# Gated delta rule in a two-layer decoder: beta and g computed inside the feed-forward, closing norms inside the schedule, a longer lookahead, and 32-wide TensorE tiles

## The chip, the cores and the metric

The kernel runs on one core of a Trainium2 chip. The engines of that core that matter here are TensorE (PE in the profile, and PEld for its weight loads), VectorE (DVE), ScalarE (ACT), GpSimd (POOL) and SyncE (SP). SP issues nearly all DMA transfers, and its queue is issued in order. The metric is the device time of one execution in microseconds, lower is better. An engine executes its own instructions in the order in which the program lists them, so a waiting instruction holds up what stands behind it on the same engine.

## The reference

Two decoder layers on `x` of shape (32, 64, 256), 2048 tokens of 256 numbers, all in float32. Each of six blocks adds its result to `x` and normalises the sum:

```python
x = _layernorm(x + _L0_attn_ref(x, ...))    # lightning attention
x = _layernorm(x + _L0_xattn_ref(x, ctx, ...))  # banded attention
x = _layernorm(x + _L0_ffn_ref(x, ...))     # feed-forward of 1024, its own layernorm inside
x = _layernorm(x + _L1_attn_ref(x, ...))    # gated delta rule
x = _layernorm(x + _L1_xattn_ref(x, ctx, ctx, ...))
x = _layernorm(x + _L1_ffn_ref(x, ...))     # 64 experts, 8 for each token
```

The change lies in the third and the fourth block. The feed-forward computes `relu(x @ up) ** 2 @ down`, adds `x @ expert` scaled by the sum of the two largest of eight logits, and normalises. The delta rule has 16 key heads and 32 value heads of 128 columns, and runs on chunks of 64 tokens; a sequence of the reshaped input is 64 tokens long too, so every chunk is a sequence and starts from a zero state:

```python
beta = sigmoid(x @ w_b)                       # 32 numbers for each token
g = -exp(a_log) * softplus(x @ w_a + dt_bias)  # 32 numbers for each token
q, k, v = split(silu(causal_conv4(x @ w_qkv)))
z = x @ w_z
# for each sequence of 64 tokens and each value head
g = cumsum(g)
decay = exp(g[i] - g[j]) for i >= j, else 0
A = -(beta * l2norm(k)) @ l2norm(k).T * decay   (strictly lower)
T = inverse(I - A)                              (64 x 64, unit lower triangular)
out = (l2norm(q) / sqrt(128) @ l2norm(k).T * decay) @ T @ (v * beta)
out = out * rsqrt(mean(out ** 2)) * norm_w * silu(z)
x_new = concat(out over heads) @ w_out
```

## The kernel before

`x` stays on the chip through the whole kernel as 16 tiles of 128 tokens; four of these tiles make a chunk `c` (512 tokens, eight sequences), of which there are four. The stages run one after the other; in the profiled execution the first attention takes 0 to 375 us, the banded attention 375 to 737, the feed-forward 737 to about 891, the delta rule with its prologue 885 to 2594, the second cross attention with the routing 2596 to 3160, and the experts the rest.

**Feed-forward (L664 to L708).** For each chunk, `make_xT` transposes `x` on TensorE (eight transposes, two ScalarE copies) into `xT[c]`; eight pairs of matmuls make `ph`, ScalarE takes its relu, GpSimd squares it into `hT` (L683). Then, for each of the four tiles, `pe` (L689) and `py` follow on TensorE, and VectorE and ScalarE combine them. Two layernorms (`x<-x,mv,rstd` is L176) close the chunk. VectorE, ScalarE and GpSimd need some microseconds for that after the last matmul; the next chunk's `make_xT` and `ph` need only their own tiles of `x`.

**Prologue of the delta rule (L711 to L808).** Constants are loaded, the two DRAM scratch buffers `tudram` are filled with zeros by SP, `make_xT` is done for all four chunks, and then beta and g are computed for all 16 tiles at once: `pba` (L770, 32 matmuls), ScalarE and VectorE element by element on 128x512, `pc` (L791, the cumulative sum), `pgT` (the same transposed), and SP stores the latter into the DRAM scratch `gdram`, from which the loop reads it back as rows to broadcast.

**Loop (L810 to L1197).** There are 64 steps, 16 key heads by four chunks. A step `s` consists of generators, each yielding before each piece of work the engine and the microseconds that the piece is expected to take:

- `conv` (L832 to L865): four of them for each step. `pp` (L850, two matmuls of 128x512), ScalarE's `acc` (L854), three VectorE additions (L859), ScalarE's silu. A first conv of a step needs step `s-5` or `s-6` done. At the first chunk of a key head SP loads its weights `wqkv`, `wz`, `wo` (two buffers).
- `decay` (for two steps at once): SP broadcasts g from `gdram`, GpSimd and ScalarE make the decay matrix.
- `matrices`: GpSimd squares (`sq`, L903), `pn` (L910, sums of squares as 32-wide matmuls of one column), VectorE's `ssum` (L916), `pk` (k with k and q), VectorE makes `am` (A transposed) and `at`; SP stores `am` to `adram`, and for each pair of steps loads the 16x16 diagonal blocks back as `w`.
- `value`: `pv` (transposes), scaled by ScalarE.
- `invert` (for two steps at once): VectorE inverts the 16x16 blocks; SP stores them into the diagonal of `tudram` (two scratch buffers), whose remaining entries are the zero fill, and then loads them back as whole 64x64 matrices `tu`, which hold T and its transpose U (four loads a step, four buffers).
- `gate`: `pz` (L1047) and ScalarE's silu.
- `delta` (L1055 to L1105): doubles the inverse twice, 16 to 32 and 32 to 64. `per_sequence` (L1067) issues one 64x64 matmul for each of 8 units and 2 sequences; the tile of a sequence lies on 64 rows and 64 columns of the array. Level one: `px` = A T, VectorE copies its lower block into `xi` (L1085, an identity otherwise), `ptu` = U xi, ScalarE copies it into T (L1090). Level two: `px` and `pm`, the product of T with `at`, VectorE copies `xi` (L1097), ScalarE `mt` (L1100), then `pm2` from `xi` and `mt`, and ScalarE's copy (L1105).
- `output` (L1108 to L1146): `po` (L1118, weights of 64 rows and 128 columns), ScalarE's square, VectorE's product with the gate, `pso`, and a power on GpSimd (L1144).
- `project` (L1148 to L1171): `py` (L1158) with the output weights, added to `x` (L1165, L1167, L1169). It sets the step done.

**What sets the order.** `scheduled` (L41 to L110) runs all of these as streams when the program is built. Each stream has so many items open at once; an item waits for its named events ("need") that others set. Of the items it can start, the function takes the engine whose next start is earliest by the costs that the generators give, and within 0.3 us prefers the stream listed first. The order that comes out is the order of each engine's instructions. Two rings stand for the PSUM banks: two for the convs, six for the rest; every "+" takes one, every "-" gives one back. `LEVELS` is (16, 32).

**After the loop (L1198 to L1205)** four layernorms, one for each chunk, and four SP stores to `xq`, from which the next stage loads its queries.

`pss` (L344) is a matmul of the first attention.

Of the kernel before, what the change touches and what calls it, by code (L numbers as in the profile page):

```python
# [23 lines left out]
LEVELS = (16, 32)  # L24
# [96 lines left out]
def decoder_kernel(ctx: ExitStack, tc: tile.TileContext, d, out):  # L121
# [539 lines left out]

    with tc.tile_pool(name="f0", bufs=1) as wp, tc.tile_pool(name="f0w", bufs=2) as sb, tc.tile_pool(
# [9 lines left out]
        for c in range(NCH):  # L672
            make_xT(c, ps)
            hT = sb.tile([P, 8, 512], FP, name="hT", tag="hT")
            for f in range(8):
# [7 lines left out]
                nc.gpsimd.tensor_tensor(hT[:, f, :], hr, hr, ALU.mult)  # L683
            ys = []
# [26 lines left out]
    with tc.tile_pool(name="g1", bufs=1) as wp, tc.tile_pool(  # L711
# [6 lines left out]
        id64 = load(wp, d["c_id64"], [P, S], "id64")  # L718
        low = load(wp, d["c_low"], [P, S], "low")
        lvl = wp.tile([P, 2, S], U8, name="lvl")  # L720
# [4 lines left out]
        adram = [dp.tile([2, 2, 8, PITCH], FP, name=f"adram{i}") for i in range(2)]  # L725
        tudram = [dp.tile([2, 2, 2, 8, PITCH], FP, name=f"tudram{i}") for i in range(2)]
        gdram = dp.tile([16, NCH, 2, 4, 2, S], FP, name="gdram")
        gall = wp.tile([P, NT, 32], FP, name="gall")

        wo16 = [wp.tile([P, 2, 16, 16], FP, name=f"wo16{i}") for i in range(2)]  # L730
        xis = [[wp.tile([P, 8, S], FP, name=f"xi{l}{i}") for i in range(2)] for l in range(2)]
        for i in range(2):
            nc.sync.dma_start(out=wo16[i].rearrange("p o j e -> p o (j e)"), in_=d["c_wid"].rearrange("p (o x) -> p o x", o=2))
        for xs_ in xis:
            for t in xs_:
                nc.gpsimd.tensor_copy(t, over(id64, 8))
# [5 lines left out]
        for c in range(NCH):  # L742
            make_xT(c, ps)


        beta = wp.tile([P, NT, 32], FP, name="beta")
        with tc.tile_pool(name="g1l", bufs=1) as tmp:
            lvlf = load(tmp, d["c_lvl"].rearrange("p (l i) -> p l i", l=2), [P, 2, S], "lvlf")
# [9 lines left out]
            tri = load(tmp, d["c_tri"], [P, P], "tri")  # L758
            wba = load(tmp, d["w_ba"].rearrange("(k p) e -> p k e", p=P), [P, 2, 64], "wba")
            dtb = load(tmp, d["dt_bias"].to_broadcast([P, 32]), [P, 32], "dtb")  # L760
            alog = load(tmp, d["a_log"].to_broadcast([P, 32]), [P, 32], "alog")
            g = tmp.tile([P, NT, 32], FP, name="g")
            aa = tmp.tile([P, NT, 32], FP, name="aa")
            ab = tmp.tile([P, NT, 32], FP, name="ab")
            for t8 in range(2):
                pba = ps.tile([P, 8, 64], FP, name="pba", tag="ps")
                for k8 in range(8):
                    t = 8 * t8 + k8
# [266 lines left out]
        def gate(s, h):  # L1035

            kh, c = steps[s]
            if h == 0:
                yield "need", ("done", s - 3)
                gates[s] = sb.tile([P, 2, 512], FP, name="z", tag="z", bufs=3)  # L1040
# [473 lines left out]
```

## Time and profile before

| quantity | value |
|---|---|
| median of 17 executions | 3691.15 us (3681.33 to 3710.32) |
| profiled execution, own time | 3693.18 us |
| profiled execution, span | 3691.5 us |
| mean granted TensorE clock over the span | 0.933 |
| PE busy | 3365.6 us (91%) |
| PE weight loads (beside PE) | 2154.2 us (58%) |
| VectorE busy | 2105.5 us (57%) |
| ScalarE busy | 1384.6 us (38%) |
| GpSimd busy | 1525.5 us (41%) |

The profile is of one execution; the medians are over executions without a profile. A line of it names the source line, the engine, the operation, output and inputs by the program's names, the size of the weights and of the stream for a matmul, the count, the busy time, the mean time of one, and the idle time of the engine just ahead of these instructions with what released them. A float32 matmul leaves two records, so counts of matmuls are twice those in the source. Ends of matmuls are modelled in the trace, so a sum over rows can exceed the time in which PE was busy. The granted clock is the share of full speed that the hardware gave TensorE. A view by windows gives the busy time of each engine for a stretch of the span.

### The profile page before, as it was taken

What the parts mean: (1) busy time and instruction counts of PE and PEld (TensorE: products, weight loads), DVE (VectorE), ACT (ScalarE), POOL (GpSimd) and SP (SyncE); (2) the same over time, 40 slices, a digit from 0 to 9 for tenths busy, and PEclk for the clock granted to TensorE, in tenths of its full rate; (3) what the DMA queues carried; (4) which work ended last, traced back from release to release, by engine and by line L of the source; (5) the groups of instructions that cost most, each with busy time, mean ns of one, the idle gap of its engine ahead of it and who ended that gap; (6) DMA issues with size and microseconds to landing.
All of it is one profiled execution on the core that took longest, in us unless ns stands there. A gap on an engine that the chain in (4) does not pass through costs nothing.

```text
span 3691.5 us, 91942 instructions
## 1 busy us (share of the span) xinstructions
PE 3365.6 (91%) x39042; PEld 2154.2 (58%) x39042; DVE 2105.5 (57%) x4316; ACT 1384.6 (38%) x2422; POOL 1525.5 (41%) x1779
## 2 busy tenths in 40 slices
PE   9999999897799999999999999999788888599990
PEld 4667566565376666766666666767444444355550
DVE  4333555544667677676677777675655555233337
ACT  1110333321545455554555555454222222133330
POOL 3322344443434344443444434443333333466663
PEclk9999899997899999998999999999878788799995
DMA  9910111001323233332332333322111111466655
GB/s 316 383 24 16 40 33 33 20 29 37 82 51 69 47 66 66 59 67 53 65 59 58 68 59 60 64 56 50 46 38 44 47 33 38 132 211 216 214 180 213
DMA packets 538700, 317.80 MB, mean 86 GB/s; under 512 B 420145, under 2 KB 498737, under 8 KB 531889
## 3 DMA queue, kind: packets, MB, share of 16 engines
q1 hardware_dynamic: 517680, 259.32, 27.3%
q0 software_dynamic: 18432, 50.49, 3.7%
q8 instruction: 308, 5.05, 0.6%
q10 hardware_dynamic: 2176, 2.10, 0.2%
q14 instruction: 104, 0.84, 0.1%
HBM read 166.42 MB, written 137.00 MB: 82 GB/s over the span
## 4 chain that ended last, share of the span: by engine, by line
PE 75%; DVE 9%; issue 5%; POOL 5%; ACT 3%; DMA 1%; another core or an unknown queue 1%; SPq 1%; POOLq 0%; DVEq 0%; ACTq 0%
PE pp L850 11%; PE py L1158 6%; PE po L531 6%; PE pz L1047 5%; PE pq L296 4%; PE sc L467 4%; PE pm L1067 3%; PE po L1118 3%; PE px L1067 3%; PE sc L499 3%; PE py L384 3%; PE py L1372 3%; PE pg L1362 2%; PE pu L1362 2%; PE ptu L1067 2%
## 5 line engine op out<-in xcount | busy, mean ns | idle before, releaser
L859 DVE SCALAR_TENSOR_TENSOR acc<-pp,cw,acc 128x504 f32<-128x504 f32 (+2 forms) x768 | 556.7, 731 | 189.4 <-ACT acc L854 159.8
L850 PE MATMUL pp<-xT,wqkv 128*128 128x512 f32 x1024 | 504.6, 618 | 22.9 <-DMA wqkv<-in_w_qkv_dram 11.7
L509 ACT ACTIVATE eT<-sc 128x768 f32<-128x768 f32 (+1 forms) x256 | 222.4, 915 | 348.0 <-PE sc L499 232.8
L477 DVE TENSOR_REDUCE mext<-sc 128x4 f32<-128x768 f32 (+1 forms) x256 | 267.6, 1087 | 101.3 <-PE sc L467 69.3
L204 POOL DMA_INDIRECT ybuf<-ye,xe x256 | 246.2, 962 | 175.7 <-DVE ye L1376 93.9
L903 POOL TENSOR_TENSOR sq<-kq 128x512 f32<-128x512 f32 x128 | 134.5, 1053 | 436.8 <-ACT kq L864 332.4
L850 PEld LDWEIGHTS pp<-xT,wqkv 128*128 128x128 f32 x1024 | 185.3, 194 | 185.6 <-issue 167.5
L1169 POOL TENSOR_TENSOR x<-x,y 128x256 f32<-128x256 f32 x256 | 184.6, 728 | 252.3 <-DVE x L1167 244.7
L467 PE MATMUL sc<-k,q 32*128 32x192 f32 (+1 forms) x2048 | 219.4, 428 | 60.4 <-issue 50.3
L1158 PE MATMUL py<-wo,og 128*128 128x256 f32 x1024 | 261.0, 393 | 2.2 <-DVE x L1167 2.2
L854 ACT ACTIVATE acc<-pp,cw 128x512 f32<-128x512 f32 x256 | 175.4, 687 | 233.5 <-PE pp L850 232.9
L1047 PE MATMUL pz<-xT,wz 128*128 128x512 f32 x512 | 246.1, 601 | 0.0
L1158 PEld LDWEIGHTS py<-wo,og 128*128 128x128 f32 x1024 | 186.9, 192 | 43.8 <-issue 16.7
L518 POOL TENSOR_SCALAR_AFFINE_SELECT eT<-eT 128x256 f32<-128x256 f32 (+1 forms) x256 | 127.6, 534 | 204.2 <-ACT eT L509 204.1
L467 PEld LDWEIGHTS sc<-k,q 32*128 32x128 f32 x2048 | 125.9, 206 | 119.5 <-issue 93.6
L531 PE MATMUL po<-eT,va 128*32 128x192 f32 (+1 forms) x2048 | 183.5, 404 | 6.5 <-issue 3.3
L499 PE MATMUL sc<-qb,k 32*128 32x192 f32 (+1 forms) x2048 | 165.3, 387 | 14.4 <-DVE mext L477 11.2
L1365 DVE TENSOR_TENSOR hT<-hT,pu 96x512 f32<-96x512 f32 x64 | 43.7, 683 | 235.5 <-PE pu L1362 224.1
L1167 DVE SCALAR_TENSOR_TENSOR x<-py,ro,x 128x256 f32<-128x256 f32 x256 | 122.5, 480 | 96.1 <-ACT y L1165 94.4
L531 PE MATMUL po<-eT,one 128*32 128x192 f32 (+1 forms) x2048 | 175.6, 389 | 0.9 <-issue 0.7
L1144 POOL TENSOR_TENSOR ro<-gvar,mhalf 128x8 f32<-128x8 f32 x64 | 105.3, 1646 | 145.2 <-DVE gvar L1139 138.1
L1165 ACT ACTIVATE y<-py,ro 128x256 f32<-128x256 f32 x256 | 120.8, 474 | 113.9 <-PE py L1158 105.7
(226 smaller groups left out, 6514.4 us busy)
## 6 DMA issues: line engine op xcount, KB each, us to landing
xbuf<-zero SPq DMA_DIRECT2D x32, 1032.0 KB
xe<-xbuf SPq DMA_DIRECT2D x64, 516.0 KB
tu<-tudram SPq DMA_DIRECT2D x256, 128.0 KB
ybuf<-zero SPq DMA_DIRECT2D x16, 1024.0 KB
de<-gdram SPq DMA_DIRECT2D x64, 256.0 KB
adram<-am SPq DMA_DIRECT2D x128, 128.0 KB
yk<-ybuf SPq DMA_DIRECT2D x16, 1024.0 KB
kk<-kT SPq DMA_DIRECT2D x32, 256.0 KB
```

What stands on the lines that cost most here:

```text
L204: i = nc.gpsimd.indirect_dma_start(out=dst, out_offset=bass.IndirectOffsetOnAxis(ap=rows, axis=0), in_=src, in_offset=None).ins
L467: nc.tensor.matmul(sc[ng // 2][:, ng % 2, qt * W : (qt + 1) * W], q32[rows, r, qt * P : (qt + 1) * P], k32[rows, r, lo[qt] : lo[qt] + W], ...
L477: nc.vector.tensor_reduce(mv4[:, 2 * hf : 2 * hf + 2, :, 8], sc[hf][:, :, : 2 * W].rearrange("p j (q l) -> p j q l", l=W), AX.X, ALU.max, ...
L499: nc.tensor.matmul(sc[ng // 2][:, ng % 2, lt * W : (lt + 1) * W], k32[rows, r, lt * P : (lt + 1) * P], qb[rows, lo[lt] : lo[lt] + W], star ...
L509: nc.scalar.activation(eT[:, 2 * hf : 2 * hf + 2].rearrange("p j h q -> p j (h q)"), sc[hf][:, :, : 2 * W], AF.Exp, scale=float(1 / np.sqr ...
L531: nc.tensor.matmul(po[32 * ng : 32 * ng + 32, i, lo[lt] : lo[lt] + W], one8[:, r, :] if i else va[:, lt, ng, 32 * r : 32 * r + 32], eT[:, ...
L850: nc.tensor.matmul(pp, weights[kh][0][:, k, i, :], xT[c][:, k, :], start=k == 0, stop=k == 1)
L859: nc.vector.scalar_tensor_tensor(acc3[:, :, sh:], pp3[:, :, : S - sh], w[:, 3 - sh : 4 - sh], acc3[:, :, sh:], ALU.mult, ALU.add,)
L1047: nc.tensor.matmul(pz, weights[kh][1][:, k, h * P : (h + 1) * P], xT[c][:, k, :], start=k == 0, stop=k == 1)
L1067: nc.tensor.matmul(dst[n, u], lhsT[n, u], rhs[n, u], start=True, stop=True)
L1158: nc.tensor.matmul(py[:, h, :], og[:, 4 * h + t].rearrange("p n i -> p (n i)"), won[:, h, :], start=True, stop=True,)
L1169: nc.gpsimd.tensor_tensor(xt, xt, y1, ALU.add)
```

## The change

1. **Beta and g** move out of the prologue into a generator `betas(c, ps)` that treats one chunk: `make_xT`'s transposes and copies for the new `x`, `pba`, the same ScalarE and VectorE chain on 128x128, `pcum`, `pgT`, and four SP stores. In the feed-forward it runs for chunk `c-1` between `ph` and `pe` of chunk `c`. For the last chunk it is a stream of the schedule. The loop's items wait for new events `xT` and `g` of their chunk. Constants for it are loaded ahead of the feed-forward's own weights on the SP queue.
2. **Closing norms** become a stream `close(c)` of the schedule, which waits for the chunk's last step; norm and store to `xq` are as before.
3. **Lookahead.** A conv needs step `s-8` done rather than `s-5` or `s-6`. `am` and `at` have eight buffers rather than six, `tu` five rather than four, the weights three rather than two, and `adram` and `tudram` three each rather than two. `invert` needs steps further back (`2m-6` and `2m+j-5`). New needs: `delta` waits for output of `s-3`, `output` for `s-2` done. Some planned costs differ, and the streams are listed in another order.
4. **Smaller TensorE tiles.** T and U are held as the 32x32 diagonal blocks alone (`tu` is 128x2x8x32, loaded by eight DMAs of 32 rows instead of four of 64). Level one uses 32x32 tiles on the array's diagonal, four for each unit, each on its own 32 rows and columns, streaming 16 columns. In level two `px2` multiplies only the one block that is not zero, two tiles for each unit, interleaved with `pm` in 32x64 tiles, four for each unit; `pm2` uses weights 64x32. `po` splits each matmul of 128 columns into two of 64. Copies of level two become plain copies of 32 rows, half on VectorE and half on ScalarE. `LEVELS` goes.

```diff
+    def betas(c, ps):
+        xT[c] = xpool.tile([P, 2, 512], FP, name=f"xT{c}", tag=f"xT{c}")
...
+        yield "pe", 1.0, "+"
+        pba = ps.tile([P, 4, 64], FP, name="pba", tag="ps")
+        for k4 in range(4):
+            for k in range(2):
+                nc.tensor.matmul(
+                    pba[:, k4, :], xT[c][:, k, k4 * P : (k4 + 1) * P], wba[:, k, :], start=k == 0, stop=k == 1
+                )
...
+        for n in range(2):
+            for hh in range(2):
+                nc.sync.dma_start(out=gdram[:, c, n, :, hh, :], in_=gT[16 * hh : 16 * hh + 16, :, n, :])
+        yield "set", ("g", c), 3.0
...
                 nc.gpsimd.tensor_tensor(hT[:, f, :], hr, hr, ALU.mult)
+            if c:
+                for _ in betas(c - 1, ps):
+                    pass
             ys = []
...
-        adram = [dp.tile([2, 2, 8, PITCH], FP, name=f"adram{i}") for i in range(2)]
-        tudram = [dp.tile([2, 2, 2, 8, PITCH], FP, name=f"tudram{i}") for i in range(2)]
+        adram = [dp.tile([2, 2, 8, PITCH], FP, name=f"adram{i}") for i in range(3)]
+        tudram = [dp.tile([2, 2, 2, 8, PITCH], FP, name=f"tudram{i}") for i in range(3)]
...
-                yield "need", ("done", s - (5 if i == 2 or c == 0 else 6))
+                yield "need", ("done", s - 8)
...
-                tu = sb.tile([P, 2, 8, S], FP, name="tu", tag="tu", bufs=4)
-                for n in range(2):
-                    for o in range(2):
+                tu = sb.tile([P, 2, 8, 32], FP, name="tu", tag="tu", bufs=5)
+                for o in range(2):
+                    for q in range(4):
+                        half = slice(32 * (q % 2), 32 * (q % 2) + 32)
                         nc.sync.dma_start(
-                            out=tu[seqs[n], o],
-                            in_=tudram[m % 2][o, j, n, :, : 64 * S].rearrange("u (r e) -> r u e", e=S),
+                            out=tu[quads[q], o],
+                            in_=tudram[m % 3][o, j, q // 2, :, : 64 * S].rearrange("u (r e) -> r u e", e=S)[half, :, half],
                         )
...
-            def per_sequence(dst, lhsT, rhs):
+            def per_block(dst, lhsT, rhs):
                 for u in range(8):
-                    for n in seqs:
-                        nc.tensor.matmul(dst[n, u], lhsT[n, u], rhs[n, u], start=True, stop=True)
+                    for q, rows in enumerate(quads):
+                        w = lhsT[rows, u]
+                        if w.shape[-1] == S:
+                            w = w[:, 32 * (q % 2) : 32 * (q % 2) + 32]
+                        nc.tensor.matmul(dst[rows, u], w, rhs[rows, u], start=True, stop=True)
...
+            px, pm = units("px2", 32), units("pm", S)
+            for u in range(8):
+                for q, rows in enumerate(quads):
+                    if q % 2 == 0:
+                        nc.tensor.matmul(px[quads[q + 1], u], am[rows, u, 32:], T[rows, u], start=True, stop=True)
+                    nc.tensor.matmul(pm[rows, u], T[rows, u], at[rows, u], start=True, stop=True)
+            yield "dve", 0.45
+            nc.vector.tensor_copy(xi[1][quads[1]], px[quads[1]])
+            yield "act", 0.4, "-"
+            nc.scalar.copy(xi[1][quads[3]], px[quads[3]])
...
-                    nc.tensor.matmul(
-                        po[n][:, u % 2 * 4 + u // 2, :], vs[seqs[n], u, :], mt[seqs[n], u, :], start=True, stop=True
-                    )
+                    for dv in seqs:
+                        nc.tensor.matmul(
+                            po[n][dv, u % 2 * 4 + u // 2, :], vs[seqs[n], u, dv], mt[seqs[n], u, :],
+                            start=True, stop=True,
+                        )
...
+        def close(c):
+            yield "need", ("done", NS - NCH + c)
...
+                (iter([betas(NCH - 1, ps)]), 1),
...
+                ((close(c) for c in range(NCH)), 1),
```

## The prediction

> **What bounds the kernel now.** I read the windows view first, by stage. Columns: stretch and length, then busy us (instructions) of PE, PEld, DVE, ACT and POOL, granted clock, DMA share, GB/s.
>
> ```profile
> 889.00:937.00 48.00, 23.94 (x107) 20.17 (x108) 9.12 (x14) 8.19 (x14) 2.31 (x4) 0.57 0.28 84
> 937.00:1040.00 103.00, 92.83 (x1084) 51.73 (x1085) 78.60 (x175) 56.30 (x91) 45.56 (x43) 0.93 0.37 75
> 1040.00:1300.00 260.00, 249.91 (x3750) 174.90 (x3751) 171.41 (x394) 130.02 (x236) 105.07 (x108) 0.94 0.29 57
> 1300.00:2400.00 1100.00, 1090.47 (x16688) 743.62 (x16685) 785.68 (x1812) 591.95 (x1057) 478.61 (x490) 0.99 0.32 62
> 2612.00:3160.00 548.00, 467.36 (x4402) 252.04 (x4401) 295.84 (x537) 154.19 (x231) 191.83 (x285) 0.82 0.13 41
> ```
>
> The delta rule's loop is 937 to 2594, 1657 us for 64 steps (25.9 each). In its middle PE is busy 1090 of 1100 us, DVE 786, ACT 592: PE bounds it and rarely waits. In 889 to 937 (beta and g) PE is half idle at clock 0.57. The groups by form price PE's small work (records, then busy us and mean ns; one matmul is two records):
>
> ```profile
> L1067 PE MATMUL px<-tu,am 64*64 64x32 f32 x4096 | 144.0, 222 | 0.8 <-ACT tu L1090 0.8
> L1118 PE MATMUL po<-mt,vs 64*128 64x64 f32 x2048 | 128.8, 275 | 0.1
> L1067 PE MATMUL pm<-at,tu 64*64 64x64 f32 x2048 | 76.0, 226 | 0.0
> L1067 PE MATMUL ptu<-xi,tu 64*64 64x32 f32 x2048 | 74.5, 228 | 9.0 <-DVE xi L1085 6.5 <-issue 1.9 <-ACT acc L854 0.2
> L1067 PE MATMUL pm<-mt,xi 64*64 64x32 f32 x2048 | 69.2, 220 | 0.4 <-DVE ssum L916 0.3
> L910 PE MATMUL pn<-ones,sq 128*32 128x1 f32 x4096 | 47.2, 172 | 5.3 <-POOL sq L903 3.8 <-issue 1.4
> L344 PE MATMUL pss<-qT,kk 64*64 64x64 f32 x2048 | 34.5, 220 | 1.9 <-POOL qT L301 0.9 <-issue 0.6 <-POOL qT L300 0.4
> ```
>
> Busy divided by records is the price of one. px costs 35.2 ns, po 62.9; pss, whose form is px's at twice the stream but which rotates over four places of the array instead of two, 16.8; pn, 32 columns wide over four column groups, 11.5. So the price falls with the width of the weights and with the number of places in rotation. The timeline shows what feeds the loop, and what one late copy does:
>
> ```profile
> 788.94 6.23 POOL L683 TENSOR_TENSOR hT<-hr 128x512 f32<-128x512 f32 x6
> 789.01 4.26 DVE L176 TENSOR_SCALAR x<-x,mv,rstd 128x256 f32<-128x256 f32 x4 [1.14 <-POOL rstd L174]
> 790.62 1.05 PE L689 MATMUL pe<-eg,xT 128*128 128x264 f32 x4
> ...
> 897.80 13.88 PE L770 MATMUL pba<-wba,xT 128*128 128x64 f32 x64 [6.13 <-issue]
> 917.73 2.04 PE L791 MATMUL pc<-g,tri 128*128 128x512 f32 x2 [6.04 <-issue]
> ...
> 936.80 3.74 PE L850 MATMUL pp<-xT,wqkv 128*128 128x512 f32 x4 [11.67 <-DMA wqkv<-in_w_qkv_dram]
> ...
> 1680.29 1.28 PE L1067 MATMUL ptu<-xi,tu 64*64 64x32 f32 x32 [1.55 <-DVE xi L1085]
> ```
>
> After that 1.55 us wait, the clock granted in 1682 to 1689 was 0.58.
>
> **The change: smaller tiles.** The loop's twelve PE groups sum to 1753.9 us of busy time, but PE was busy 1625.5 us there by the windows: ends are modelled and blocks overlap, so each us of rows is 0.927 us of stream. The five groups replaced are 144.0+128.8+76.0+74.5+69.2 = 492.5 us of rows. Per step the new ones are: px and ptu of level one, 64 records each, 32 wide, four places (pn's row: 11.5 ns); px2 with pm, 96 records, four places, streams of 32 and 64 (pss: 16.8); pm2, 32 records, 32 wide but two places (twice pn: 23); po, 64 records of pss's form (16.8). Level one differs from pn in using four row groups and streaming 16, so it lies between pn and pss; with no reason for either I take the middle, 14.1 ns. Over 64 steps: 8192 x 14.1 = 115.5, 6144 x 16.8 = 103.2, 2048 x 23 = 47.1, 4096 x 16.8 = 68.8; together 334.6. Removed 157.9 of rows, 146 us of stream. Bounds: level one at pn's price gives 166 us; at 23 ns (only two places work together) 78 us; if every 32-wide record kept px's 35.2 ns, 16384 x 35.2 + 68.8 = 645.5, a loss of 142 us.
>
> A rule speaks against this edit. The Trainium skill, page TensorEngine Tiling (Array Packing), Performance Considerations, says that each matmul carries some 60 cycles and warns against taking the tiling from a dimension that is already small; at the 2.4 GHz of its TensorE page that is about 25 ns, as an estimate. For 320 records a step it would make 8.0 us where the old rows have 7.7, so a sum of about 3765. pn's 11.5 ns, streaming one column, contradicts it.
>
> **Waits in the loop.** The old order runs level one of two steps together, so one's copy hides under the other's matmuls; still PE and PEld waited 20.7 us for L1085 (14.2 and 6.5, 0.32 us a step). In the order of the changed kernel's instructions, level one of a step mostly stands alone; between its px and ptu a quarter of the steps have under 1.2 us of other PE work by these rows. DVE's copy takes 0.43 us now and may stand behind a 0.73 us conv. I double the wait (+21 us), and add six waits like the one at 1680, each with some 7 us at half clock (+24): +45. Bounds: zero, as eight steps in flight may also remove waits, and the 83 us of the rival below.
>
> **Beta and g.** Before, PE's last feed-forward matmul ends near 876 and the first conv starts at 936.8: 61 us. Afterwards betas of chunk c-1 stand on PE between ph and pe of chunk c, in order, so pe and py queue behind them. In chunk 1: x of chunk 0 is normalised at 793.3 (789.01+4.26); eight transposes and two copies as at 775.5 to 777.2, 1.7; pba, a quarter of 13.88 at half clock, 1.7 at full; the ACT and DVE chain took 6.0 us (911.7 to 917.7) with operands four times as wide, of which 1.28 is a table load, so some 3.8; pc and pgT 1.4. pe starts near 802 instead of 790.6; as hT itself was late (795.2), some 11 us are lost, 11 to 14 with a slower clock, three times: +37. At the end x of chunk 3 needs the same 14.6 us (876.3 to 890.9); then the SP queue sends the constants, three zero fills instead of two and the weights. The fills (2.1 MB) kept the DMA engines busy to about 896.5; the third adds 3 us, and weights landed 4.2 us after issue. The first conv comes some 30 us after the feed-forward, not 61: -31. Four loads ahead of up on SP: +2. Sum +8; bounds -10 (the chain half hidden) and +20.
>
> **The rest** I cost at nothing. Closing norms: DVE ran chunk 0's among the loop's last steps before, and the four xq stores keep their places on SP; x1's first scores waited for q, 2594 to 2612, behind them (bounds -10, +3). tu in eight DMAs of half the size: 256 more SP issues at 633 ns are 162 us more of a queue with 1657 us; in the order tu is issued over 14 us of PE work ahead of its delta in all but a few steps, and that lead covers the 2.5 us later issue. If the cover goes, adram, w and the weights behind tu on SP are late and each delta waits 2.5 us. Copies: DVE loses two 0.43 us copies a step and gains three smaller ones, about +0.2 us, ACT +0.25, under DVE's 71% and ACT's 54%. Third weight buffer, triple adram: cover only.
>
> **Sum** against the profiled run's 3693.2 us (2 over the median of 3691.2): 3693 - 146 + 45 + 8 = 3600.
>
> **Rivals.** *Half of it:* 32-wide tiles work in pairs: 3693 - 78 + 45 + 8 = 3668. For: no row has four row groups and four column groups at once. Against: pn and pss. *More:* pn's price, waits as now, chain hidden: 3693 - 166 + 5 + 0 = 3532. For: row width alone would set pn's price. Against: order of PE in the feed-forward. *Slower:* PE is no longer fed. DVE's and ACT's work does not shrink, and waits for xi over a microsecond cost clock. If PE is busy as in x1 (2612 to 3160: 85.3%, clock 0.82), 1625.5 - 146 = 1480 us need 1735, 78 us more than 1657: 3693 + 78 + 8 = 3779. It decides from 138 us of new waits and slow clock on, 2.2 us a step. For: x1 shows it. Against: DVE's 786 us of 1100 leave a quarter of a shorter step free.
>
> **How the numbers follow.** Main case 0.60, its own range 3550 to 3645; half 0.17; more 0.10; slower 0.12, nearly half of it beyond 3720; the remaining 0.01 is the 35.2 ns case, above 3800. About 0.2% (7 us) is what a measurement can tell from no change. The main case, more, and all of half but 0.02 are faster: 0.85; within 0.2%: 0.02; slower 0.13. The range cuts the lower edge of more and the cases above 3685: 3535 to 3685 leaves 0.18 out.
>
> **What would show it.** Per record: level one 11 to 17 ns, px2 and pm about 17, po about 17, pm2 about 23 (23 or more in level one is the half case). The loop near 1550 us, PE over 94% busy in its middle at clock over 0.95; ptu's waits for xi about 40 us. In the feed-forward, PE idle before pba and pc in three chunks; the first conv near 945. I am wrong if the loop's PE share falls under 90%, or small records cost over 23 ns.

## The result and the profile after

The changed kernel takes 3742.3 us (median of 8, 3739.81 to 3750.59) against 3691.4 us before: a ratio of 1.0143, 95% interval 1.0129 to 1.0156. It is 1.4% slower where 2.5% faster was forecast, and lies outside the stated range. The profiled execution took 3743.96 us, with a span of 3742.2 us.

By stages, from the two traces: the first conv of the loop starts at 946.7 us (before 936.8), the loop takes 1707 us (before 1657), and from its last matmul to the end 1088 us pass (before 1098). The loop was to lose 101 us, by 146 us less stream and 45 us more waits, and gained 50. The windows view of the changed kernel for the stretches shown of before (columns as there):

```profile
889.00:937.00 48.00, 30.31 (x126) 25.18 (x125) 17.30 (x52) 8.20 (x15) 11.66 (x16) 0.71 0.18 65
937.00:1040.00 103.00, 79.04 (x759) 38.52 (x760) 67.43 (x148) 52.59 (x82) 43.87 (x43) 0.86 0.38 92
1040.00:1300.00 260.00, 230.33 (x5364) 150.72 (x5364) 182.16 (x433) 132.56 (x247) 102.18 (x103) 0.89 0.29 51
1300.00:2400.00 1100.00, 998.68 (x21537) 639.16 (x21530) 785.20 (x1814) 577.67 (x1069) 463.32 (x475) 0.93 0.27 50
2612.00:3160.00 548.00, 464.75 (x4785) 258.40 (x4788) 306.95 (x582) 159.78 (x254) 196.92 (x292) 0.83 0.14 42
```

In the middle of the loop PE's busy time fell from 1090 to 999 of 1100 us, and the granted clock from 0.99 to 0.93. VectorE, ScalarE and GpSimd do as much in the stretch as before (785, 578 and 463 us), so none of them has become the bound. The groups by form of the replaced matmuls:

```profile
L1127 PE MATMUL pm<-at,tu 32*32 32x64 f32 x4096 | 92.8, 237 | 23.8 <-issue 22.4 <-DVE acc L883 1.3
L1160 PE MATMUL po<-mt,vs 64*64 64x64 f32 x4096 | 82.7, 227 | 2.8 <-DVE og L1172 2.3 <-DVE mt L1143 0.3
L1126 PE MATMUL px<-tu,am 32*32 32x32 f32 x2048 | 81.2, 207 | 18.3 <-issue 17.3 <-ACT tu L1119 0.2
L1101 PE MATMUL ptu<-xi,tu 32*32 32x16 f32 x4096 | 55.5, 187 | 36.7 <-issue 18.9 <-DVE xi L1114 16.3 <-ACT vs L1015 1.2
L1101 PE MATMUL px<-tu,am 32*32 32x16 f32 x4096 | 49.1, 182 | 8.2 <-issue 6.2 <-DMA tu<-tudram 2.0
L1139 PE MATMUL pm<-mt,xi 64*32 64x32 f32 x2048 | 48.4, 197 | 7.0 <-issue 4.7 <-DVE xi L1129 1.9
```

The rows sum to 409.7 us (before 492.5), but the rows of `px` (L1126) and `pm` (L1127) cover the same time: their matmuls alternate, and by the instruction records of the trace PE was busy with the two together for 93.5 us, not 174.0. Counted so, the groups come to 329 us, as cheap as the 334.6 expected. What is new stands behind the bar: idle time in front of small matmuls that is put down to "issue", which means that PE waited for nothing that the profile shows as a semaphore. The view of PE's waits over the changed kernel's loop, the longest first (us in total, times, longest):

```profile
PE pp L874 <- DVE acc L883: 22.4, 11, 2.7
PE pm L1127 <- issue: 22.4, 18, 2.5
PE ptu L1101 <- issue: 18.9, 23, 2.5
PE px L1126 <- issue: 17.3, 12, 2.2
PE ptu L1101 <- DVE xi L1114: 16.3, 11, 2.4
PE pso L1179 <- ACT osq L1170: 11.9, 12, 2.6
PE pp L874 <- DMA wqkv<-in_w_qkv_dram: 10.1, 1, 10.1
```

All waits of the kind "issue", called unnamed from here on, come to 86.5 us in the loop (before 3.3); waits with a named releaser to 78.5 without the first load of weights (before 27.2). The stretches at half clock cost 129 us (before 38), counted as their length times one minus the clock.

Such a wait without a name, in the changed kernel's timeline:

```profile
1341.54 1.14 PE L1160 MATMUL po<-mt,vs 64*64 64x64 f32 x58
1342.61 0.71 PE L935 MATMUL pn<-ones,sq 128*32 128x1 f32 x64
1343.30 0.72 PE L1101 MATMUL ptu<-xi,tu 32*32 32x16 f32 x64
1343.95 0.48 PE L1201 MATMUL py<-wo,og 128*128 128x256 f32 x1
1345.54 1.78 PE L1201 MATMUL py<-wo,og 128*128 128x256 f32 x7 [1.11 <-issue]
```

Three small blocks run one after the other, and then PE stops after the first of eight records of `py`, a block whose operands have all arrived. No tile explains a stop in the middle of a block. A lead is the profile's list of DMA queues (packets, MB, share of 16 engines). In the kernel before it has

```profile
q8 instruction: 308, 5.05, 0.6%
```

and in the changed kernel

```profile
q8 instruction: 372, 6.09, 0.7%
```

Each transfer of this queue is 16,384 bytes. The kernel before has 39,042 matmul and as many weight-load records, 78,084 in all; 64 bytes for each make 5.00 MB. The changed one has 94,480, or 6.05 MB. So the queue carries PE's own instructions, in pages of 256, which are 128 matmul records or 64 float32 matmuls. In the changed loop 51 waits of at least 0.5 us stand inside a block (the same line before and after the wait). Of these, 48 ended between 1.1 and 1.7 us after a page of this queue had landed. Of the unnamed waits as a whole 84 us end so, of the 78.5 us of named ones 9; only 9% of the loop's time lies that far behind a landing, so this is no accident. The theory for the experiments, the supply theory, is that PE runs through its pages faster than they arrive. The rivals: that the longer lookahead and the new order of streams put PE's work in a worse order (waits for data), and that narrow tiles lower the clock by themselves.

### The profile page after: what moved, and what is told of

It is laid out like the page before. It is cut to its first block, busy times and chain, and to the rows that moved or that the text cites. A ratio compares the mean times of both kernels' runs of the same rounds, so it can differ in the third digit from the quotient of the medians.

```text
span 3742.2 us, 108758 instructions
## 1 busy us (share of the span) xinstructions
PE 3278.2 (88%) x47240; PEld 2029.0 (54%) x47240; DVE 2130.3 (57%) x4400; ACT 1400.8 (37%) x2503; POOL 1522.6 (41%) x1779
## 4 chain that ended last, share of the span: by engine, by line
PE 66%; DVE 17%; issue 7%; POOL 4%; ACT 3%; DMA 2%; another core or an unknown queue 1%; SPq 0%; POOLq 0%; DVEq 0%; ACTq 0%
PE pp L874 9%; PE py L1201 6%; PE po L530 5%; DVE acc L883 5%; PE pq L295 4%; PE sc L466 4%; PE py L1437 3%; PE sc L498 3%; PE py L383 3%; DVE wtmp L1033 3%; PE pg L1427 3%; PE pu L1427 3%; DVE w L1036 3%; PE pz L1076 2%; PE pk L968 2%
## 5 line engine op out<-in xcount | busy, mean ns | idle before, releaser
L883 DVE SCALAR_TENSOR_TENSOR acc<-pp,cw,acc 128x496 f32<-128x496 f32 (+2 forms) x768 | 555.8, 730 | 185.4 <-ACT acc L878 176.7
L874 PE MATMUL pp<-xT,wqkv 128*128 128x512 f32 x1024 | 521.7, 638 | 35.6 <-DVE acc L883 22.4
L874 PEld LDWEIGHTS pp<-xT,wqkv 128*128 128x128 f32 x1024 | 195.6, 201 | 209.4 <-issue 172.6
L1201 PE MATMUL py<-wo,og 128*128 128x256 f32 x1024 | 295.6, 427 | 4.7 <-DVE og L1172 2.7
L1076 PE MATMUL pz<-xT,wz 128*128 128x512 f32 x512 | 238.3, 597 | 0.0
L1201 PEld LDWEIGHTS py<-wo,og 128*128 128x128 f32 x1024 | 204.0, 211 | 56.9 <-issue 25.9
```

The lines of the kernel that those rows point to most:

```text
L874: nc.tensor.matmul(pp, weights[kh][0][:, k, i, :], xT[c][:, k, :], start=k == 0, stop=k == 1)
L883: nc.vector.scalar_tensor_tensor(acc3[:, :, sh:], pp3[:, :, : S - sh], w[:, 3 - sh : 4 - sh], acc3[:, :, sh:], ALU.mult, ALU.add,)
L1076: nc.tensor.matmul(pz, weights[kh][1][:, k, h * P : (h + 1) * P], xT[c][:, k, :], start=k == 0, stop=k == 1)
L1201: nc.tensor.matmul(py[:, h, :], og[:, 4 * h + t].rearrange("p n i -> p (n i)"), won[:, h, :], start=True, stop=True,)
```

## The experiments

All comparisons of time are with the kernel before, run beside it on the same chip. The columns for the loop come from each run's profiled execution: unnamed waits ("issue"), named waits, and clock loss (stretches at half clock). The wait for the first load of weights is in neither; in e3 and e4 the view gives it as "issue" (6.0 and 7.5 us). Clock that is lost during a wait is in two columns; by the traces this overlap is 1.5 us before, 13.6 in the changed kernel and at most 22 (e6).

| kernel | median us (before beside it) | ratio, 95% interval | loop | unnamed | named | clock loss |
|---|---|---|---|---|---|---|
| before | 3691.4 | | 1657 | 3 | 27 | 38 |
| changed | 3742.3 (3691.4) | 1.0143 (1.0129 to 1.0156) | 1707 | 87 | 79 | 129 |
| e2 tiles alone | 3657.9 (3690.1) | 0.9920 (0.9894 to 0.9946) | 1630 | 68 | 60 | 87 |
| e3 beta, g and norms alone | 3706.7 (3690.1) | 1.0045 (1.0030 to 1.0061) | 1672 | 7 | 27 | 49 |
| e4 all but the lookahead part | 3668.2 (3690.1) | 0.9950 (0.9936 to 0.9964) | 1641 | 70 | 64 | 94 |
| e5 changed, old stream order | 3693.2 (3682.1) | 1.0030 (1.0013 to 1.0047) | 1657 | 58 | 80 | 95 |
| e6 changed, old distance of convs | 3789.8 (3682.1) | 1.0303 (1.0277 to 1.0330) | 1755 | 85 | 104 | 165 |
| e7 tiles, paced | 3566.0 (3682.1) | 0.9686 (0.9659 to 0.9713) | 1548 | 12 | 66 | 33 |
| e8 changed, paced | 3637.0 (3682.1) | 0.9879 (0.9850 to 0.9908) | 1605 | 11 | 93 | 56 |
| e9 tiles, planned costs only | 3621.9 (3693.2) | 0.9805 (0.9788 to 0.9822) | 1603 | 59 | 47 | 75 |
| e10 before, paced | 3654.2 (3693.2) | 0.9886 (0.9863 to 0.9909) | 1632 | 0 | 13 | 26 |
| e11 narrow | 3597.3 (3693.2) | 0.9743 (0.9721 to 0.9766) | 1574 | 13 | 26 | 28 |
| e12 narrow, paced | 3506.5 (3575.5) | 0.9804 (0.9781 to 0.9827) | 1589 | 2 | 48 | 37 |

### e1: the price of small matmuls and of their instructions

```diff
+        def blocks32(n):
+            for u in range(n):
+                rows = quads[u % 4]
+                nc.tensor.matmul(mb[rows, 16 * (u // 4 % 8) : 16 * (u // 4 % 8) + 16],
+                    x[rows, 0, 32 * (u % 4) : 32 * (u % 4) + 32], x[rows, 1, :16], start=True, stop=True)
...
+        big(32)
+        blocks32(320)
+        big(32)
+        blocks32wide(320)
+        big(32)
+        blocks32half(320)
+        big(32)
+        blocks64(160)
+        big(32)
+        for _ in range(10):
+            blocks32(32)
+            big(2)
```

> The kernel before, with blocks of matmuls into a scratch bank added between the transposes and beta (its time is of no interest). Blocks: 320 matmuls of 32x32 weights streaming 16 columns over the four diagonal places; 320 of the same streaming 64 columns; 320 as the first but in bf16; 160 of 64x64 streaming 32; ten times 32 of the first kind with 2 matmuls of 128x512 between. 32 matmuls of 128x512 stand ahead of each block. Supply theory (PE runs out of instructions: the page's instruction queue q8 carried 5.05 MB for 78,084 PE records before and 6.09 MB for 94,480 after, 64 bytes for each record, in transfers of 16,384 bytes, so 256 records or 64 float32 matmuls each; in the loop after the change no two transfers start closer than 3.3 us): the first block starts at about 24 ns a matmul, then stops for 1 to 2.5 us about every 64 matmuls, 50 to 56 ns a matmul on average; the block of 64 columns comes to the same average; the bf16 block, where a matmul has half the records, to about half, 28 ns; the 64x64 block, 58 ns in the old loop, has hardly a stop; the interleaved block has none. Width theory (the price lies in the array, and small tiles themselves lower the clock): no stops, an even price through each block, and a lower granted clock in the interleaved block as well.

The timeline of the five blocks (each with `big`, the 128x512 matmuls, before it):

```profile
917.04 2.16 PE L760 MATMUL mb<-x 32*32 32x16 f32 x236
921.56 1.90 PE L760 MATMUL mb<-x 32*32 32x16 f32 x128 [2.36 <-issue]
925.31 1.90 PE L760 MATMUL mb<-x 32*32 32x16 f32 x128 [1.84 <-issue]
929.05 1.91 PE L760 MATMUL mb<-x 32*32 32x16 f32 x128 [1.84 <-issue]
...
967.50 1.99 PE L765 MATMUL mb<-x 32*32 32x64 f32 x128 [1.48 <-issue]
970.97 1.99 PE L765 MATMUL mb<-x 32*32 32x64 f32 x128 [1.48 <-issue]
...
1006.92 2.06 PE L770 MATMUL mb<-xh 32*32 32x16 bf16 x235
1011.70 0.84 PE L770 MATMUL mb<-xh 32*32 32x16 bf16 x85 [2.72 <-issue]
...
1042.39 9.52 PE L775 MATMUL mb<-x 64*64 64x32 f32 x320
...
1079.50 0.73 PE L760 MATMUL mb<-x 32*32 32x16 f32 x64
1080.16 1.98 PE L755 MATMUL wide<-x 128*128 128x512 f32 x4
1082.07 0.73 PE L760 MATMUL mb<-x 32*32 32x16 f32 x64
```

This is the supply theory's picture. A small matmul itself is nearly free: in the interleaved block 64 records start within 0.55 us, 8.7 ns each. But after 236 records PE stops, and from then on after every 128 records exactly, one page. From page to page it takes 3.47 us at full clock (967.50, 970.97) and 3.75 in the first block, where the clock was at half from 921.5 to 938.5; so long rows of 128 records took no less than 3.47 us on average, 27 ns a record, with streams of 64 columns as with 16. The bf16 block has one record for a matmul and stops once, at record 235; its 320 matmuls end before a second stop could come, so it took 17 ns a matmul rather than the 28 expected. The 64x64 block needs 29.2 ns a record, 3.74 us a page, and so just keeps pace. The interleaved block has no stop, and the windows view gives it full clock, below the first two blocks' rows:

```profile
917.00:932.90 15.90, 8.30 (x641) 7.84 (x640) 0.00 (x0) 0.00 (x0) 0.00 (x0) 0.64 0.02 4
963.40:979.20 15.80, 9.88 (x641) 9.20 (x640) 0.00 (x0) 0.00 (x0) 0.00 (x0) 1.00 0.02 5
...
1079.50:1103.20 23.70, 23.70 (x677) 12.32 (x676) 0.00 (x0) 0.00 (x0) 0.00 (x0) 1.00 0.01 3
```

The width theory falls with it: narrow tiles run at clock 1.00 where nothing stops them.

### e2, e3, e4: the parts alone

e2 has the kernel before with only part 4 (the new `delta`, `output`, `tu` loads and constants). e3 has only parts 1 and 2. e4 undoes part 3 in the changed kernel, in essence:

```diff
-                yield "need", ("done", s - 8)
+                yield "need", ("done", s - (5 if i == 2 or c == 0 else 6))
...
-            yield "need", ("output", s - 3)
...
-            yield "need", ("done", s - 2)
...
-            yield "dve", 2.2, "-"
+            yield "dve", 2.3, "-"
...
-            yield "pool", 1.65
+            yield "pool", 1.05
...
+                ((project(s, t2) for s in each for t2 in range(2)), 2),
                 ((delta(s) for s in each), 2),
                 ((decay(m) for m in range(NS // 2)), 1),
-                ((project(s, t2) for s in each for t2 in range(2)), 2),
                 (convs(), 2),
-                ((invert(m) for m in range(NS // 2)), 1),
                 ((gate(s, h) for s in each for h in range(2)), 1),
+                ((invert(m) for m in range(NS // 2)), 1),
```

> The kernel before with the smaller tiles alone (the delta and output generators, the tu loads in blocks and their constants of the changed kernel; lookahead, buffers, stream order, prologue and closing norms of before). Supply theory: PE's waits in the loop without a named releaser stay at 60 to 90 us and cost clock, against some 146 us less stream; 3640 to 3720 us. Order theory (the longer lookahead and the new stream order put PE's work in a worse order): those waits are under 15 us, and the time is 3560 to 3620.

> The kernel before with beta and g by chunks inside the feed-forward and the closing norms in the schedule alone (64-wide tiles, lookahead, buffers and stream order of before). By the stages of the two traces the first conv came 9.9 us later and the part behind the loop was 9.7 us shorter, so 3680 to 3700 us, the loop at 1650 to 1665. If the work moved into the loop disturbs it, the loop is over 1680 and the time over 3710.

> The changed kernel with the lookahead, the buffers, the planned costs of conv and of the power, and the stream order of before. Supply theory: the waits without a named releaser stay (70 to 100 us in the loop), the time is within 25 us of the changed kernel's 3742. Order theory: waits for named releasers fall from 80 to about 30 us in the loop, the clock rises to 0.95 or more, and the time is under 3690.

The tiles alone gain 32 us; 68 us of unnamed waits are there without any change of the lookahead, as the supply theory has it. Beta, g and norms cost 17 us, between the two branches of the expectation: the first conv came 6.9 us later and the part behind the loop was 12 us shorter, but the loop was 16 us longer. Its unnamed waits are 4 us and its clock loss 11 us above those of before; the beta of the last chunk and the norms now run in it. e4 falls between the theories and says that both have a part: the unnamed waits stay (70 us), but the ratio is 0.995 against 1.0143, a difference of 71 us. So part 3, which the prediction cost at nothing, is what makes the change a loss. (The profiled execution of e4 is the slowest of its ten, 16 us over their median, so that its loop is rather shorter than the table says.)

### e5 and e6: what in the lookahead

e5 puts the list of streams of the changed kernel back into the old order, as in the last lines of e4's diff, and does nothing else. e6 puts back the distance alone:

```diff
-                yield "need", ("done", s - 8)
+                yield "need", ("done", s - (5 if i == 2 or c == 0 else 6))
```

The 120 us in the expectation of e5 are an estimate: PE's records in program order, each at the price measured inside blocks at full clock, and wherever 128 of them take less than 3.5 us, the rest added as a stop.

> The changed kernel with the old order of the streams in the list of the schedule alone (lookahead of eight, buffers, needs and costs as changed). Two theories of what in the lookahead part costs the 74 us between the changed kernel and the one with the old lookahead. Bursts: the new order of streams puts small blocks side by side, and PE runs out of instructions more often. Counting each kernel's TensorE records in program order, with the full-clock prices of the trace and at least 3.5 us for every 128 records, the stops come to 120 us for the changed kernel, 93 for the old lookahead and 62 here; so the waits without a named releaser fall from 86 us to some 50, the clock loss in the loop from 129 us to under 95, and the time to 3650 to 3690. Lookahead: convs eight steps ahead take PE early and leave the end of the loop without cover; then the stream order changes little: 3720 to 3760, and 80 us from the last conv to the end of the loop.

> The changed kernel with a conv waiting for step s-5 or s-6, as before, in place of s-8, and nothing else. Bursts: the count gives 131 us of stops, no fewer than the changed kernel's 120, so 3725 to 3790 us. Lookahead: the loop returns to about 1640 us, and the time to 3660 to 3690.

The distance of the convs is not the cause: with the old one the loop gets 48 us longer still, and the time is at the upper end of what the burst theory expected. The order of the streams in the list is: the old order alone takes the unnamed waits from 87 to 58 us, the clock loss from 129 to 95 and the ratio from 1.0143 to 1.0030, which is 42 us; the time is three us over the range expected of bursts. The named waits do not move (79 and 80), so what was gained is waits for instructions and clock. The 29 us that still lie between e5 and e4 (needs, buffers, planned costs and distance together) were not taken apart.

### e7 to e10: keeping account of instructions

If the stops come from small blocks side by side, a planner that knows this should remove them with the same instructions. e7 is e2 with an allowance of records in `scheduled` (at most 56, refilled at 30 a us); each piece on PE names how many it has, and the small blocks get the shorter planned costs of the traces:

```diff
         def start(self):
-            engine, _, flags = (*self.step, "")[:3]
+            engine, us, flags = (*self.step, "")[:3]
             t = max(self.ready, free.get(engine, 0.0))
+            if engine == "pe":
+                need = (self.step[3] if len(self.step) > 3 else 0) - us * RATE
+                t = max(t, tokens[1] + (need - tokens[0]) / RATE)
...
             free[engine] = t + us
+            if engine == "pe":
+                tokens[0] = min(CAP, tokens[0] + (t - tokens[1]) * RATE) + us * RATE - (self.step[3] if len(self.step) > 3 else 0)
+                tokens[1] = t + us
+                tokens[0] = min(CAP, tokens[0])
...
-            yield "pe", 1.75, "+c"
+            yield "pe", 1.75, "+c", 4
...
-            yield "pe", 1.03, "+t"
+            yield "pe", 0.7, "+t", 64
```

> The kernel with the smaller tiles alone (run e2), whose planner also keeps account of TensorE's records: each piece names how many it has, an allowance of 56 refills at 30 a us, and a piece that lacks them starts later, so that the planner puts a conv, a gate or a projection between small blocks. The planned costs of the small blocks are set to the trace's prices (0.7 us for level one, 0.68 for the sums). Same instructions, another order. Supply theory: the count gives 22 us of stops against 95, so the waits without a named releaser fall from 68 us to under 30, the clock loss from 87 to under 60, and the time from 3658 to 3560 to 3610. If small tiles lower the clock themselves, the clock loss stays at 80 or more and the time over 3630.

> The changed kernel, whole, with the same account of records in its planner and the same planned costs of small blocks. Supply theory: the count gives 10 us of stops against 120; the waits without a named releaser fall from 86 us to under 25, the clock loss from 129 to under 70, the time from 3742 to 3580 to 3640. If waits for VectorE and ScalarE carry the loss, those waits stay at 80 us or grow, and the time stays over 3690.

The time of e7 is 3566 us, 3.1% under the kernel before. The waits and the windows of its loop:

```profile
PE px L1106 <- ACT tu L1099: 25.4, 25, 2.5
PE pp L859 <- DMA wqkv<-in_w_qkv_dram: 13.1, 1, 13.1
PE pv L994 <- ACT vv L873: 12.7, 25, 0.5
PE pp L859 <- DVE w L1019: 8.2, 17, 0.7
PE pm L1107 <- issue: 5.7, 6, 2.4
```

```profile
934.50:2482.30 1547.80, 1468.56 (x32768) 916.40 (x32768) 1166.10 (x2782) 884.89 (x1631) 702.66 (x719) 0.98 0.30 54
1300.00:2400.00 1100.00, 1057.38 (x23983) 659.27 (x23982) 842.49 (x2010) 640.99 (x1185) 509.35 (x522) 0.99 0.30 55
```

The clock is back at 0.99, with the same narrow tiles and as many records, and the unnamed waits are 12 us. The timeline shows the new order:

```profile
1707.29 1.88 PE L859 MATMUL pp<-xT,wqkv 128*128 128x512 f32 x4
1709.10 0.73 PE L1081 MATMUL px<-tu,am 32*32 32x16 f32 x64
1709.76 1.98 PE L859 MATMUL pp<-xT,wqkv 128*128 128x512 f32 x4
1711.67 0.73 PE L1081 MATMUL ptu<-xi,tu 32*32 32x16 f32 x64
1712.33 1.98 PE L1057 MATMUL pz<-xT,wz 128*128 128x512 f32 x4
```

The big matmul between the two small blocks gives the next page time to arrive, and covers the copy between them as well. e8 shows the same on the whole change: the unnamed waits fall from 87 to 11 us, the clock loss from 129 to 56, the ratio from 1.0143 to 0.9879. It stays 71 us behind e7, with 27 us more named waits, 23 more clock loss and a first conv 13 us later. Two controls:

> Control for the paced kernel (run e7): the smaller tiles alone with its planned costs for the small blocks (0.7 us in level one, 1.25, 0.68 for the sums) and no account of records. Supply theory: the count gives 78 us of stops, the waits without a named releaser stay at 45 to 75 us in the loop, and the time at 3620 to 3670. If the better costs and not the pacing made the gain, the time is 3555 to 3590.

> Second control: the kernel before, 64-wide tiles, with the account of records in its planner (56 and 30 a us), its planned costs else kept but for 0.68 us for the two sums. Supply theory: there is next to nothing to remove (3 us of waits without a named releaser in the loop, the count gives 8 us of stops before and 1 after), so within 15 us of the kernel before, 3665 to 3700. If pacing helps by something else (fewer waits for VectorE and ScalarE, a better clock whatever the tiles), over 30 us faster.

Better planned costs alone (e9) take the ratio from e2's 0.992 to 0.981, at the near end of what the supply theory gave, and leave 59 us of unnamed waits; the account takes it on to 0.969. About half of the gain is each one's. e10 missed: the supply theory expected next to nothing, and pacing gained 39 us on the old tiles, where there was hardly a stop to remove. By the profiles 24 us of this lie in the loop: its named waits fell from 27 to 13 us (the 6.5 us for `xi` are gone) and its clock loss from 38 to 26. So spreading small blocks among large ones can also hide copies. In e7 this does not show as a sum: against e9 its named waits rose from 47 to 66 us, while the unnamed ones fell by 47 and the clock loss by 42, so that what the account gained there is stops for instructions and clock.

### e11 and e12: fewer records

e11 is the kernel before with only those smaller tiles that need few more instructions: in level two weights of 64x32 for `px` and `pm2`, and `po` split. A step then has 416 records, against 384 before and 512 in the changed kernel (the expectation below has 448).

```diff
-            px = units("px", 1)
-            per_sequence(px, am, columns(T, 1))
+            px = ps.tile([P, 8, S // 2], FP, name="px2", tag="ps")
+            for u in range(8):
+                for n in range(2):
+                    nc.tensor.matmul(px[quads[2 * n + 1], u], am[seqs[n], u, 32:], T[seqs[n], u, :32], start=True, stop=True)
...
-            per_sequence(pm, xi[1], mt[:, :, S // 2 :])
+            for u in range(8):
+                for n in range(2):
+                    nc.tensor.matmul(
+                        pm[quads[2 * n], u], xi[1][seqs[n], u, :32], mt[seqs[n], u, 32:], start=True, stop=True
+                    )
```

> The kernel before with only those tile changes that need few more instructions: in level two px and pm2 with weights of 64x32 for the half that is not known already, pm as before, level one as before (64x64), po split in two. 640 records more than before's 384 in a step become 448 in place of 512. By prices at full clock a step loses 0.33 + 0.34 + 0.79 us, 93 us in all; the count gives 17 us of stops against 8. Supply theory: 3590 to 3640, with under 25 us of waits without a named releaser. If every small tile costs more than its stream whatever the number of records (as a drop of the clock), the gain is half of it: over 3640.

> The kernel of run e11 (few more records, 64x64 tiles in level one) with the account of records in its planner (56 and 30 a us, planned costs as in e11 but 0.68 for the sums). It has 68 us more stream at full clock in the loop than the paced small tiles of run e7 (1497 against 1429), but fewer records to supply, 26,624 against 32,768. If pacing mainly removes stops for instructions, there are few left to remove here (12.6 us) and it stays within 15 us of e11's 3597. If pacing also keeps the clock and the other waits down, as in run e10 (39 us with hardly a stop to remove), 3555 to 3580.

e11 came out as expected: 96 us, more than half of what the whole set of tiles has in stream (163, below), with 13 us of unnamed waits and the clock loss below that of before. e12 ran on a chip where the kernel before took 3575.5 us and the part behind the loop some 105 us less, so that only its ratio and its loop can be compared: with the interval of e11's ratio below its own, and a loop of 1589 us against 1574, pacing brought nothing here and cost a little: 22 us by the ratios, somewhat more than the 15 us of the first branch. Its unnamed waits fell from 13 to 2 us, its named ones rose from 26 to 48. That is nearer to the branch in which pacing mainly removes stops than to e10; what decides whether spreading hides copies or exposes them was not found.

## Why the prediction was wrong

**What bounds the loop** was read rightly: PE did, and after the change none of the other engines took its place.

**Smaller tiles, the stream.** Right. By the prices inside blocks at full clock the loop's stream fell from 1591 to 1429 us, and by what is left of the loop without waits and clock loss from 1590 to 1427: 163 us where 146 was summed. Level one cost 12.0 and 13.6 ns a record (14.1 assumed, between pn and pss), `pm2` 23.6 (23) and `po` 20.2 (16.8); half-clock time is in these rows, and e7's `po`, at a clock of 0.98, is 19.4. `px2` with `pm` came to 15.2 (16.8 assumed), the 93.5 us in which either ran, over 6144 records. Their rows must not be added, as e7's timeline shows: a record lasts over 0.2 us, and the next starts some 0.01 us after it.

```profile
1715.31 0.24 PE L1107 MATMUL pm<-at,tu 32*32 32x64 f32 x2
1715.32 0.21 PE L1106 MATMUL px<-tu,am 32*32 32x32 f32 x1
```

**Waits in the loop, the step that failed.** The prediction took +45 us, bounded by zero and 83. Measured were 83 us more unnamed waits, 51 more named ones and 91 more clock loss, 225 us, less 12 us by which these overlap more than before: with the stream, -163 + 225 - 12 is the +50 of the loop. The named waits alone lie within the bounds. The unnamed ones were in no step and in no rival, and with them came most of the clock: in e8, where they are down to 11 us while the named ones are 14 us more, the clock loss is 56 us rather than 129. Two figures of the step do not follow from its own numbers: six waits with 7 us at half clock are 21 us, not 24, and the rival's 3779 us stand for 78 + 146 = 224 us of waits and clock, not 83. The slower rival, with its 224 us, had the right outcome and the size, by the wrong mechanism in the main: PE was no longer fed, but with instructions more than with data. That its sum came near the measured time is luck. It could have been seen: the profile listed the instruction queue with its 5.05 MB, the change adds some 8,200 matmul records in the loop to 24,576, and pn and pss, the two rows that set the new prices, come in blocks of 64 and 128 records, fewer than the 172 to 236 that ran before the first stop in e1.

**The rule weighed there.** The Trainium skill, page TensorEngine Tiling (Array Packing), section Performance Considerations, has some 60 cycles for a matmul, which would have made about 3765. The sum came near the 3742 measured, but not by that price: e1 shows 8.7 ns a record in a short block, 17 ns a matmul, and 27 ns a record only where pages have to be awaited. The prediction also charged the 25 ns to each record; the page speaks of a matmul, which leaves two records here, and by matmuls the same estimate would be 4.0 us a step rather than 8.0. The same skill's page Runtime: NRT & Kernel Launch, section Instruction fetch mechanics, states that the sequencer fetches instructions in blocks of 16 KiB, each of 256 instructions, while it runs the block before, and that this is mostly hidden by the pace at which instructions are issued. The size agrees with the trace (16,384 bytes). That it is hidden holds for the old tiles (3.3 us of unnamed waits in the loop) and not for these (86.5).

**"The rest I cost at nothing", the second step that failed.** Buffers and lookahead were called cover only, and the new order of the streams was not costed at all. Part 3 costs 71 us by the ratios (1.0143 against e4's 0.995), 42 of them by the order of a list (e5). The prediction read the new order of PE's instructions for too little work between one small block and its successor, but not for small blocks in a row.

**Beta and g.** The mechanism was right. In the changed kernel `pba` starts at 794.28, `pcum` waits 3.71 us for the chain on ScalarE and VectorE (3.8 expected), and the first `pe` follows at 804.18 (near 802 expected). The first conv started at 946.7 (near 945 expected):

```profile
794.28 3.62 PE L695 MATMUL pba<-wba,xT 128*128 128x64 f32 x16 [0.24 <-ACT xT L684]
801.61 0.80 PE L720 MATMUL pcum<-g,tri 128*128 128x128 f32 x2 [3.71 <-DVE g L714]
802.34 1.92 PE L725 MATMUL pgT<-tri,g 128*32 128x128 f32 x8
804.18 1.63 PE L767 MATMUL pe<-eg,xT 128*128 128x264 f32 x4
```

The +8 us were +9.9. What was missed is the 16 us by which e3's loop was longer.

**Closing norms and the small loads.** The part behind the loop was 10 us shorter, at the bound named (-10) where nothing was taken. The tu loads in eight pieces (a quarter of the old size, 32 KB against 128, where the prediction has half) were hidden as argued: PE waited for them once, 2.0 us.

**The range and the chances.** The measured time lies 57 us above the range, in the slower case that was given 0.12. Its point of decision, 138 us of new waits and slow clock, was passed, with 225 us less the overlap of 12.

## What to carry to other kernels

Count TensorE's instructions as a resource of its own: here a page of 128 matmul records (64 float32 matmuls) came every 3.47 us at best in e1, and in the changed loop no two transfers started closer than 3.2 us, so small tiles paid only as far as large matmuls stood between their blocks, and a cheap row with few records a block says nothing of three such blocks in a row. An order written by a planner should be charged for this before tiles are cut: the same tiles gained 0.8% in an order that did not know of it and 3.1% when the planner kept account and had the right costs for the small blocks (the costs alone: 2.0%), and the whole change lost 1.4% without both and gained 1.2% with them. Where that is not possible, the tiles that shrink the stream and add few records (e11: 2.6%) brought most of the gain, with 13 us of unnamed waits.

## What the runs showed of the hardware

- Instruction pages: 16,384 bytes, 128 float32 matmul records with their weight loads; after large matmuls 172 to 236 records ran before the first stop, then one page every 3.47 us (3.75 at half clock). 48 of the 51 stops inside blocks of the changed loop ended 1.1 to 1.7 us after a page had landed.
- A 32x32 float32 matmul over the four diagonal places takes 8.7 ns a record from start to start in a block of 64, with 16 columns; by busy time (0.73 us for the block, 11.4 a record), which is what the prediction's 14.1 stood for, it is dearer, since the end of the block counts too.
- The clock: the first stop of e1, 2.36 us, was followed by 17 us at half clock (with three more stops of 1.56 to 1.84 us in them), while four stops of 1.48 us, one every 3.47 us, left it at 1.00; in the kernel before, one wait of 1.55 us (at 1680) was followed by half clock. Narrow tiles without stops ran at full clock (1.00 in e1's interleaved block).
